# Alternating transposes and v2 products on TensorE in a fused graph attention layer, with VectorE's work in another order

## Chip, cores and metric

The kernel runs on one core of a Trainium2 chip. The metric is device time in microseconds (us) of one execution; lower is better.

## What is computed

The reference is a graph attention layer over 384 nodes with 1024 features and 16 heads of 64, with a residual:

```python
h = relu(layernorm(x))
q = h @ wq.T + bq;  k = h @ wk.T + bk;  v = h @ wv.T + bv
q2 = heads(q @ wiq.T + biq); k2 = heads(k @ wik.T + bik); v2 = heads(v @ wiv.T + biv)
scores = q2 @ k2.T / 8 + mask          # mask: from the edge list, -inf where there is no edge
out = softmax(scores) @ v2
return x + out @ wo.T + bo
```

`mask[src, dst]` is a softplus weight chosen by the edge's type.

## The kernel before

Matrices are held as a high and a low half (fp32r, or fp16 in the attention part), so that one product of the reference is three on TensorE (`mm3`: high x high, high x low, low x high). Weights arrive in 56 chunks of 512 KB: `load` issues a chunk's transfer on the queue of SyncE (SP), `split_hi` rounds it on ScalarE, `split_lo` subtracts on VectorE or GpSimd. The first 32 chunks (v, q, v2, k) are done in a stage of their own, up to about 160 us. What follows is the stage that the change touches.

It is a loop of steps `i`, in an order written out by hand; each engine does its own instructions in the order in which the code issues them. There are 48 score tiles, three (128 rows each) for each of 16 heads; tile `i` is tile `t = i % 3` of head `h = i // 3`. On its way a tile passes through these functions, each some steps behind the one before:

- `do_S`: two score products into a PSUM bank `s` (two such banks).
- `do_ttr` (VectorE): adds the mask, takes the row minimum of the negative, writes tile `e` (six buffers).
- `do_exp` (ScalarE), `do_norm` (reciprocal on VectorE; the scaling on GpSimd for `t` = 1, 2).
- Tiles with `t` = 0: `do_high` (ScalarE) and `do_low` (VectorE) write two fp16 planes and `do_turn` transposes them by a DMA on SP's queue.
- Tiles with `t` = 1, 2: `do_T` transposes on TensorE (three transposes of 128x128, bank `t`, two banks), `do_pt` takes the result to fp16 halves (high on ScalarE, low on VectorE).
- `do_A`: six v2 products of a head (fp16, 384 wide) into the one bank `a`; `do_ao` (ScalarE, then VectorE) takes them out, `do_aos` (ScalarE, then GpSimd) splits a pair of heads for the output product.

Between these, `fill` puts other products on TensorE, by a credit of 7.9 (later 8) per step. First come those of `fill_qk`: 16 chunks of q2 and k2 weights, 24 products each. When a chunk begins, `qk_head` is queued as a task and run at the end of the step: it issues a load, splits the weights two chunks on, and calls `qk_done`, which takes the finished chunk before out of PSUM (`nat`: ScalarE high, VectorE low) and issues four DMAs on SP's queue. Then come the products of `fill_o`, the output matrix: six groups (a half row of a node tile each), each in two halves of k with one bank `g` per half (three banks, taken in turn; two groups of the second half use bank `s`). `ysum` adds a finished half to the residual on VectorE and so frees its bank; `flush_y` issues the sums that are due. `OREADY` is the earliest step for the products of a k. `wo_prep` splits a chunk of the output weights in the steps of `WSTEPS`.

Of the kernel before, what the change touches and what calls it, by code (L numbers as in the profile page):

```python
# [1 line left out]

# [23 lines left out]
def gnn_kernel(ctx: ExitStack, tc: tile.TileContext, x, edges, erows, etw, wq, wk, wv, wiq, wik, wiv, wo,  # L26
# [20 lines left out]
    def bank(tag):  # L47
        return psum.tile([128, 512], F32, tag=tag, name=tag, bufs={"g": 3, "a": 1}.get(tag, 2))
# [14 lines left out]
    def load(w):  # L63
        if w >= NCH:
            return
        n, m = chunks[w]
        raw[w] = wpool.tile([128, D], F32, tag="raw", name="raw", bufs=4)
        nc.sync.dma_start(raw[w], W[n][m])

    def split_hi(w, dst=None, dve=False):  # L70
        if w >= NCH:
            return
        if dst is None:
            t = wpool.tile([128, 2, D], F32R, tag="whl", name="whl", bufs=4)
            dst = (t[:, 0, :], t[:, 1, :])
        whl[w] = dst
        if dve:
            nc.vector.tensor_copy(dst[0], raw[w])
        else:
            nc.scalar.activation(dst[0], raw[w], AF.Copy)  # L80

    def split_lo(w, eng=None):
        if w < NCH:
            hi, lo = whl[w]
            (eng or nc.vector).tensor_tensor(lo, raw[w], hi.bitcast(F32), OP.subtract)  # L85
# [155 lines left out]
    def mask_select(g):  # L241

        nc.vector.copy_predicated(ma, mbt[g].bitcast(I32), mbt[g])
# [148 lines left out]
    w = 0  # L392
# [203 lines left out]
            tasks.pop(0)()  # L596

    def qk_head(w):
        first = w - W0 < 3
        if not first:  # L600
            load(w + 5)
            split_hi(w + 2)
        if pendq:
            pendq.pop(0)()
        if 0 < w - W0 < NTAB:
            mask_select(w - W0)
        if first:
            split_hi(w + 2)
        split_lo(w + 2, nc.gpsimd if (w + 2) % 2 == PAR else None)
        if first:  # L610
            load(w + 5)
        if w == W0:
            mask_select(0)

# [17 lines left out]
    W0 = 32  # L632
    WO = NCH - 8

    LT, LA = 5, 7
    DT = (0,)
    PRE, RATE, RATE_O, RATE_E = 84, 7.9, 8, 8
    WSTEPS = (37, 40, 42, 44, 47, 51)
# [17 lines left out]
    def omm(t, h, k, c=(0, 512)):  # L656
        hi, lo = (a[:, h * 512 + c[0]:h * 512 + c[1]] for a in whl[WO + k])
        mm3(oacc[t, h][:, c[0]:c[1]], ao[:, 0, k, t * 128:(t + 1) * 128], ao[:, 1, k, t * 128:(t + 1) * 128],
            hi, lo, k in (0, KH), k in (KH - 1, KT - 1))

    OT = [(0, 0), (0, 1), (1, 0), (1, 1), (2, 0), (2, 1)]
    OREADY = 17
    now = [-1]
    wready = [0, 0] + [99] * 6

    def ysum(a, c=(0, 512)):
        t, h = OT[a]
        y = xb[t][:, h * 512 + c[0]:h * 512 + c[1]]
        nc.vector.tensor_tensor(y, oacc[t, h][:, c[0]:c[1]], y, OP.add)
        return y  # L670

    ysums = []

    def flush_y():
        while ysums:
            ysum(ysums.pop(0))

    def fill_o():


        first = [(0, 0), (0, 1), (1, 0), (1, 1), (2, 0), (2, 1)]
        first += [(a, k) for k in (2, 3) for a in range(3)] + [(a, k) for a in range(3, 6) for k in range(KH)]
        for a, k in first:
            while now[0] < wready[k] or now[0] < 6 * k + OREADY:
                yield 0
            if k == 0:
                flush_y()
                oacc[OT[a]] = bank("g")
            omm(*OT[a], k)
            if k == KH - 1:  # L690
                ysums.append(a)
            yield 4
        bank_step = (0, 0, 0, 49, 50)
        todo = [(a, k) for k in range(KH, 7) for a in range(5)]
        while todo:
            ready = [q for q in todo if now[0] >= max(6 * q[1] + OREADY, wready[q[1]], bank_step[q[0]])]
            if not ready:
                yield 0
                continue
            a, k = ready[0]  # L700
            todo.remove(ready[0])
            if k == KH:
                flush_y()
                oacc[OT[a]] = bank("gggss"[a])
            omm(*OT[a], k)
            yield 4

    st_ps, es, sts, tps, avs, aof = {}, {}, {}, {}, {}, {}
    S = 48

    def do_S(i):
        h, t = divmod(i, 3)
        p, o = divmod(h, 2)
        qs, ks = stacks["q", p], stacks["k", p]
        ps = st_ps[i] = bank("s")
        for s in range(2):
            nc.tensor.matmul(ps[:, :N], qs[:, o, t * 128:(t + 1) * 128], ks[:, o, s, :], start=(s == 0), stop=(s == 1))  # L717
# [7 lines left out]
    def do_exp(i):  # L725
        s = sts[i]
        nc.scalar.activation(es[i], es[i], AF.Exp, bias=s[:, 0:1], scale=-1.0, accum_out=s[:, 1:2])  # L727
# [20 lines left out]
    def do_high(i):  # L748
        planes[i] = plv[i // 3 % 3]
        nc.scalar.activation(planes[i][:, 0, :], es[i], AF.Copy, scale=sts[i][:, 2:3])  # L750

    def do_low(i):
        pl = planes[i]
        nc.vector.scalar_tensor_tensor(pl[:, 1, :], es.pop(i), sts[i][:, 2:3], pl[:, 0, :], op0=OP.mult, op1=OP.subtract)  # L754
# [3 lines left out]
        nc.sync.dma_start_transpose(ptv[h % 3][:, :, t * 128:(t + 1) * 128],  # L758
                                    planes.pop(i).rearrange("p a n -> p (a n)"))

    def do_T(i):
        ps = tps[i] = bank("t")
        for k in range(3):
            nc.tensor.transpose(ps[:, k * 128:(k + 1) * 128], es[i][:, k * 128:(k + 1) * 128], ident)  # L764

    def do_pt(i):
        h, t = divmod(i, 3)
        pt = ptv[h % 3]
        hi, lo = (pt[:, s * 3:s * 3 + 3, t * 128:(t + 1) * 128] for s in range(2))
        pv = tps.pop(i)[:, :N].rearrange("p (k n) -> p k n", k=3)  # L770
        nc.scalar.activation(hi, pv, AF.Copy, scale=PSC)  # L771
        nc.vector.scalar_tensor_tensor(lo, pv, PSC, hi, op0=OP.mult, op1=OP.subtract)  # L772

    def do_A(h):
        p, o = divmod(h, 2)
        ps = avs[h] = bank("a")
        for k in range(3):
            for s in range(2):
                nc.tensor.matmul(ps[:, :N], vhl[:, k, h, :, :], ptv[h % 3][:, 3 * s + k, :],  # L779
                                 start=(k == 0 and s == 0), stop=(k == 2 and s == 1))  # L780

    def do_ao(h):
        p, o = divmod(h, 2)
        if o == 0:
            aof[p] = work.tile([128, N], F32, tag="aof", name="aof")
        tmp = work.tile([128, N], F32, tag="aot", name="aot", bufs=1)
        ps = avs.pop(h)
        m, l = slice(o * 64, o * 64 + 64), slice(64 - o * 64, 128 - o * 64)
        nc.scalar.activation(tmp[m, :], ps[l, :N], AF.Identity, scale=down[l], bias=bc[m, 40 + p:41 + p])
        nc.vector.scalar_tensor_tensor(aof[p][m, :], ps[m, :N], down[m], tmp[m, :], op0=OP.mult, op1=OP.add)  # L790

    def do_aos(h):
        p = h // 2
        nc.scalar.activation(ao[:, 0, p, :], aof[p], AF.Copy)
        nc.gpsimd.tensor_tensor(ao[:, 1, p, :], aof[p], ao[:, 0, p, :].bitcast(F32), OP.subtract)
# [4 lines left out]
    def fill(n):  # L800
        credit[0] += n
        while credit[0] > 0 and gens:
            try:
                c = next(gens[0])
            except StopIteration:
                gens.pop(0)
                continue
            if c == 0:
                credit[0] = 0.0
                return  # L810
            credit[0] -= c
# [1 line left out]
    fill(PRE)  # L813
    pt_setup()
    wp = 2
    for i in range(S + LA + 4):
        now[0] = i
        r = RATE if len(gens) == 2 else RATE_O if i < S else RATE_E
        fill(r / 2)
        if i < S:  # L820
            do_S(i)
        fill(r / 2)
        if 0 <= i - 1 < S:
            do_ttr(i - 1)
        flush_y()
        if 0 <= i - 2 < S:
            do_exp(i - 2)
        if 0 <= i - 3 < S:
            do_norm(i - 3)
            if (i - 3) % 3 in DT:  # L830
                do_high(i - 3)
        if 0 <= i - LT < S and (i - LT) % 3 not in DT:
            do_T(i - LT)
        j = i - LA
        if j >= 2 and (j - 2) % 3 == 0 and (j - 2) // 3 < 16:
            do_A((j - 2) // 3)
        if 0 <= i - 4 < S and (i - 4) % 3 in DT:
            do_low(i - 4)
        if 0 <= i - LT - 1 < S and (i - LT - 1) % 3 not in DT:
            do_pt(i - LT - 1)  # L840
        if j >= 3 and (j - 3) % 3 == 0 and (j - 3) // 3 < 16:
            do_ao((j - 3) // 3)
        if j >= 4 and (j - 4) % 6 == 3:
            do_aos((j - 4) // 3)
        run_tasks()
        if 0 <= i - 4 < S and (i - 4) % 3 in DT:
            do_turn(i - 4)
        if i in WSTEPS:
            wo_prep(wp)
            wready[wp] = i + 2  # L850
            wp += 1
    while gens:
        now[0] = 999
        fill(999)


    def finish(a, c=(0, 512)):
# [51 lines left out]
```

## Time and profile before

| | |
|---|---|
| median of 3 runs | 297.39 us (297.25 to 299.25) |
| profiled execution | 297.12 us |
| its span, first to last instruction | 295.4 us |
| TensorE matmul, weight load | 287.1, 264.6 us busy |
| VectorE | 214.9 us busy |
| ScalarE | 160.4 us busy |
| GpSimd | 155.6 us busy |
| granted TensorE clock | 1.000 |

In the profile PE is TensorE's matmul, PEld its weight load, DVE VectorE, ACT ScalarE, POOL GpSimd, SP SyncE. A row of a timeline gives the start in us from the beginning of the span, the time taken, engine, source line, operation, what is written and read, shapes and count; in brackets stands the engine's idle time before it and what ended it. Rows of a source line or tile give the shortest, median and longest duration in ns. Matmuls are pipelined: one starts before the one ahead of it has ended, so their spacing is read from the starts.

### The profile page before, as it was taken

How to read it: one execution, taken by the hardware profiler on the slowest of the kernel's cores; microseconds unless marked ns; L12 is line 12 of the kernel's file. 1: busy time of each engine (PE TensorE's matmuls, PEld its weight loads, DVE VectorE, ACT ScalarE, POOL GpSimd, SP SyncE). 2: the span in 40 equal slices, each digit the busy share in tenths (PEclk: the TensorE clock that was granted, in tenths of full speed). 3: DMA queues.
4: the chain of work that ended last, by engine and by line, in shares of the span. 5: the costliest groups of instructions: out<-in, count | busy, mean ns of one | idle time of the engine just before them, and what ended most of it. 6: DMA issues, size and time to landing. Idle time of an engine off the chain costs nothing.

```text
span 295.4 us, 4837 instructions
## 1 busy us (share of the span) xinstructions
PE 287.1 (97%) x1610; PEld 264.6 (90%) x1610; DVE 214.9 (73%) x509; ACT 160.4 (54%) x291; POOL 155.6 (53%) x153
## 2 busy tenths in 40 slices
PE   6999999999999999999999999999999999989995
PEld 5999999999988889999999999898999998758774
DVE  4958986667754453999875778888888878598723
ACT  3884644234422124335635668787878777459510
POOL 4766666445766888990023445362635357475310
PEclk9999999999999999999999999999999999999999
DMA  7799867982464331386449999777788867811105
GB/s 270 252 327 411 288 192 266 288 279 74 145 214 141 107 118 65 89 275 233 142 126 236 255 249 202 189 175 194 181 201 179 200 159 162 213 29 27 27 2 213
DMA packets 33305, 54.60 MB, mean 185 GB/s; under 512 B 17408, under 2 KB 20992, under 8 KB 33280
## 3 DMA queue, kind: packets, MB, share of 16 engines
q1 hardware_dynamic: 30896, 51.90, 60.8%
q0 software_dynamic: 2064, 1.80, 2.1%
q10 hardware_dynamic: 320, 0.59, 0.8%
q8 instruction: 13, 0.21, 0.3%
q14 instruction: 12, 0.10, 0.1%
HBM read 38.30 MB, written 3.39 MB: 141 GB/s over the span
## 4 chain that ended last, share of the span: by engine, by line
PE 88%; ACT 5%; issue 3%; DVE 2%; DMA 1%; POOL 0%; ACTq 0%
PE g L375 20%; PE g L373 20%; PE g L374 20%; PE s L717 5%; PE a L779 5%; PE t L764 3%; PE s L375 2%; PE s L373 2%; PE s L374 2%; PE g L422 2%; PE t L375 2%; PE t L373 2%; PE t L374 2%; DMA g<-in_x_dram 1%; ACT whl L80 1%
## 5 line engine op out<-in xcount | busy, mean ns | idle before, releaser
L373 PE MATMUL g<-g,whl 128*128 128x384 f32 x312 | 106.8, 342 | 0.0
L375 PE MATMUL g<-g,whl 128*128 128x384 f32 x312 | 104.5, 335 | 0.0
L374 PE MATMUL g<-g,whl 128*128 128x384 f32 x312 | 104.3, 334 | 0.0
L230 POOL DMA_INDIRECT tab<-val,idx x51 | 58.0, 1138 | 33.4 <-issue 11.5
L80 ACT ACTIVATE whl<-raw 128x1024 fp32r<-128x1024 f32 x51 | 53.6, 1053 | 30.0 <-PE g L375 21.1
L85 DVE TENSOR_TENSOR whl<-raw,whl 128x1024 fp32r<-128x1024 f32 x41 | 54.2, 1321 | 17.4 <-ACT whl L80 15.1
L373 PEld LDWEIGHTS g<-g,whl 128*128 128x128 f32 x312 | 58.6, 188 | 0.7
L375 PEld LDWEIGHTS g<-g,whl 128*128 128x128 f32 x312 | 58.6, 188 | 0.3 <-POOL whl L85 0.3
L374 PEld LDWEIGHTS g<-g,whl 128*128 128x128 f32 x312 | 58.6, 188 | 0.0
L744 POOL TENSOR_TENSOR e<-e,s 128x384 f32<-128x384 f32 x32 | 27.6, 864 | 39.0 <-DVE s L740 37.5
L85 POOL TENSOR_TENSOR whl<-raw,whl 128x1024 fp32r<-128x1024 f32 x11 | 26.5, 2411 | 36.8 <-ACT whl L80 33.3
L389 ACT ACTIVATE g<-f,bc 128x384 fp32r<-128x384 f32 x24 | 14.8, 618 | 53.5 <-DVE f L388 39.6
L727 ACT ACTIVATE e<-e,s 128x384 f32<-128x384 f32 x48 | 29.2, 607 | 8.7 <-DVE s L723 7.6
L723 DVE CUSTOM_DVE_ANT_0 e<-s,ma 128x384 f32<-128x384 f32 x48 | 26.4, 551 | 3.0 <-PE s L717 3.0
L717 PE MATMUL s<-ks,qs 128*128 128x384 f32 x96 | 25.1, 342 | 2.3 <-DVE s L723 2.3
L388 DVE TENSOR_TENSOR f<-g,rrow 128x384 f32<-128x384 f32 x24 | 13.3, 553 | 18.0 <-PE g L375 12.0
L717 PEld LDWEIGHTS s<-ks,qs 128*128 128x128 f32 x96 | 17.0, 188 | 5.0 <-DVE s L723 4.2
L384 DVE SCALAR_TENSOR_TENSOR nat<-g,bc,nat 128x384 fp32r<-128x384 f32 x16 | 9.9, 617 | 14.7 <-ACT nat L383 13.6
L754 DVE SCALAR_TENSOR_TENSOR pt<-e,s,pt 128x384 f16<-128x384 f32 x16 | 19.0, 1187 | 1.4 <-ACT pt L750 0.2
L772 DVE SCALAR_TENSOR_TENSOR pt<-t,pt 128x384 f16<-128x384 f32 x32 | 17.4, 544 | 1.9 <-ACT pt L771 1.9
L779 PE MATMUL a<-pt,vhl 128*128 128x384 f16 x96 | 18.2, 326 | 0.0
L390 DVE SCALAR_TENSOR_TENSOR g<-f,bc,g 128x384 fp32r<-128x384 f32 x24 | 16.7, 700 | 0.7 <-ACT g L389 0.7
(166 smaller groups left out, 446.3 us busy)
## 6 DMA issues: line engine op xcount, KB each, us to landing
ks<-nat SPq DMA_DIRECT2D x30, 192.0 KB
raw<-in_wv_dram SPq DMA_DIRECT2D x8, 512.0 KB
raw<-in_wq_dram SPq DMA_DIRECT2D x8, 512.0 KB
raw<-in_wiv_dram SPq DMA_DIRECT2D x8, 512.0 KB
raw<-in_wk_dram SPq DMA_DIRECT2D x8, 512.0 KB
raw<-in_wiq_dram SPq DMA_DIRECT2D x8, 512.0 KB
raw<-in_wik_dram SPq DMA_DIRECT2D x8, 512.0 KB
raw<-in_wo_dram SPq DMA_DIRECT2D x8, 512.0 KB
```

The costliest lines, as they stand in the source:

```text
L80: nc.scalar.activation(dst[0], raw[w], AF.Copy)
L85: (eng or nc.vector).tensor_tensor(lo, raw[w], hi.bitcast(F32), OP.subtract)
L230: nc.gpsimd.indirect_dma_start(out=tabs[c // RNG], out_offset=bass.IndirectOffsetOnAxis(ap=idx[:, c:c + 1], axis=0), in_=val[:, c:c + 1], ...
L373: nc.tensor.matmul(ps, lhi, rhi, start=first, stop=False)
L374: nc.tensor.matmul(ps, lhi, rlo, start=False, stop=False)
L375: nc.tensor.matmul(ps, llo, rhi, start=False, stop=last)
L717: nc.tensor.matmul(ps[:, :N], qs[:, o, t * 128:(t + 1) * 128], ks[:, o, s, :], start=(s == 0), stop=(s == 1))
L723: nc.vector.tensor_tensor_reduce(e, st_ps.pop(i)[:, :N], ma[:, t, :], -0.125, 3.0e38, OP.add, OP.min, s[:, 0:1])
L727: nc.scalar.activation(es[i], es[i], AF.Exp, bias=s[:, 0:1], scale=-1.0, accum_out=s[:, 1:2])
L744: nc.gpsimd.tensor_tensor(es[i], es[i], s[:, 2:3].to_broadcast([128, N]), OP.mult)
L754: nc.vector.scalar_tensor_tensor(pl[:, 1, :], es.pop(i), sts[i][:, 2:3], pl[:, 0, :], op0=OP.mult, op1=OP.subtract)
L779: nc.tensor.matmul(ps[:, :N], vhl[:, k, h, :, :], ptv[h % 3][:, 3 * s + k, :], start=(k == 0 and s == 0), stop=(k == 2 and s == 1))
```

## The change

Tiles 3h+1 and 3h+2 are both transposed in step 3h+7 (before: 3h+6 and 3h+7), and the v2 products of the head before, which move from step 3h+6 to 3h+7 of this count, are issued in turn with them: transpose, product, transpose, product, six of each. The last head keeps the steps it had. `do_pt` for both tiles and `do_ao` follow in the step after. `do_low` moves ahead of `do_exp` and `do_norm`. The sums of output groups are issued one at a time, just before the bank that they free is taken again, rather than all in the step in which they are due. In `qk_head`, `qk_done` comes first, then the split, and the load last, for every chunk (before: for the first three alone). `OREADY` rises by one.

```diff
     def qk_head(w):
-        first = w - W0 < 3
-        if not first:
-            load(w + 5)
-            split_hi(w + 2)
         if pendq:
             pendq.pop(0)()
         if 0 < w - W0 < NTAB:
             mask_select(w - W0)
-        if first:
-            split_hi(w + 2)
+        split_hi(w + 2)
         split_lo(w + 2, nc.gpsimd if (w + 2) % 2 == PAR else None)
-        if first:
-            load(w + 5)
+        load(w + 5)
...
-    LT, LA = 5, 7
...
-    OREADY = 17
+    OREADY = 18
...
-    def flush_y():
-        while ysums:
+    def flush_y(n=6):
+        for _ in range(min(n, len(ysums))):
             ysum(ysums.pop(0))
...
             if k == 0:
-                flush_y()
+                flush_y(1)
                 oacc[OT[a]] = bank("g")
...
             if k == KH:
-                flush_y()
+                flush_y(1)
                 oacc[OT[a]] = bank("gggss"[a])
...
-    def do_T(i):
+    def turn_mm(i):
         ps = tps[i] = bank("t")
         for k in range(3):
             nc.tensor.transpose(ps[:, k * 128:(k + 1) * 128], es[i][:, k * 128:(k + 1) * 128], ident)
+            yield
...
-    def do_A(h):
-        p, o = divmod(h, 2)
+    def av_mm(h):
         ps = avs[h] = bank("a")
         for k in range(3):
             for s in range(2):
                 nc.tensor.matmul(ps[:, :N], vhl[:, k, h, :, :], ptv[h % 3][:, 3 * s + k, :],
                                  start=(k == 0 and s == 0), stop=(k == 2 and s == 1))
+                yield
+
+    def turns_and_av(tiles, heads):
+        a, b = ([g(x) for x in xs] for g, xs in ((turn_mm, tiles), (av_mm, heads)))
+        a, b = (itertools.chain(*x) for x in (a, b))
+        end = object()
+        while True:
+            x, y = next(a, end), next(b, end)
+            if x is end and y is end:
+                return
...
+    t_at, a_at = {}, {}
+    for h in range(16):
+        for t in (1, 2):
+            t_at.setdefault(3 * h + 7 if h < 15 else 3 * h + 5 + t, []).append(3 * h + t)
+        a_at[3 * h + 10 if h < 15 else 3 * h + 9] = h
-    for i in range(S + LA + 4):
+    for i in range(S + 11):
...
             do_ttr(i - 1)
-        flush_y()
+        if 0 <= i - 4 < S and (i - 4) % 3 in DT:
+            do_low(i - 4)
         if 0 <= i - 2 < S:
             do_exp(i - 2)
         if 0 <= i - 3 < S:
             do_norm(i - 3)
             if (i - 3) % 3 in DT:
                 do_high(i - 3)
-        if 0 <= i - LT < S and (i - LT) % 3 not in DT:
-            do_T(i - LT)
-        j = i - LA
-        if j >= 2 and (j - 2) % 3 == 0 and (j - 2) // 3 < 16:
-            do_A((j - 2) // 3)
-        if 0 <= i - 4 < S and (i - 4) % 3 in DT:
-            do_low(i - 4)
-        if 0 <= i - LT - 1 < S and (i - LT - 1) % 3 not in DT:
-            do_pt(i - LT - 1)
-        if j >= 3 and (j - 3) % 3 == 0 and (j - 3) // 3 < 16:
-            do_ao((j - 3) // 3)
-        if j >= 4 and (j - 4) % 6 == 3:
-            do_aos((j - 4) // 3)
+        turns_and_av(t_at.get(i, []), [a_at[i]] if i in a_at else [])
+        for x in t_at.get(i - 1, []):
+            do_pt(x)
+        if i - 1 in a_at:
+            do_ao(a_at[i - 1])
+        if a_at.get(i - 2, 0) % 2:
+            do_aos(a_at[i - 2])
         run_tasks()
...
     while gens:
         now[0] = 999
         fill(999)
+    flush_y()
```

More of the change, by code (lines that the diff above doesn't have):

```diff
@@ L1 @@
+import itertools
 from contextlib import ExitStack
```

## Prediction

> **What bounds the kernel now.** I read the page's engine shares and the chain first, then the timeline of TensorE around every place where two starts are too far apart, then VectorE and ScalarE at those places.
>
> ```profile
> span 295.4 us, 4837 instructions
> PE 287.1 (97%) x1610; PEld 264.6 (90%) x1610; DVE 214.9 (73%) x509; ACT 160.4 (54%) x291; POOL 155.6 (53%) x153
> PE 88%; ACT 5%; issue 3%; DVE 2%; DMA 1%; POOL 0%; ACTq 0%
> ```
>
> TensorE sets the end. A change can win only by giving it less work or by taking out its gaps. The profiled execution took 297.12 us, 1.7 around its span of 295.4; the median of the runs is 297.39. My sum is made against 297.12. A measurement of this kernel tells about 1% (3.0 us) from no change.
>
> The gaps, on TensorE in order of time:
>
> ```profile
> 185.86 0.33 PE L375 MATMUL g<-g,whl 128*128 128x384 f32 x1
> 186.03 0.51 PE L717 MATMUL s<-ks,qs 128*128 128x384 f32 x2
> ...
> 189.49 0.34 PE L375 MATMUL g<-g,whl 128*128 128x384 f32 x1
> 190.24 0.61 PE L717 MATMUL s<-ks,qs 128*128 128x384 f32 x2 [0.42 <-DVE s L723]
> ...
> 203.89 0.34 PE L375 MATMUL g<-g,whl 128*128 128x384 f32 x1
> 204.65 0.61 PE L717 MATMUL s<-ks,qs 128*128 128x384 f32 x2 [0.42 <-DVE s L723]
> ...
> 218.29 0.34 PE L375 MATMUL g<-g,whl 128*128 128x384 f32 x1
> 218.53 0.62 PE L717 MATMUL s<-ks,qs 128*128 128x384 f32 x2
> ...
> 232.17 0.34 PE L375 MATMUL g<-g,whl 128*128 128x384 f32 x1
> 232.42 0.62 PE L717 MATMUL s<-ks,qs 128*128 128x384 f32 x2
> ...
> 252.63 0.40 PE L373 MATMUL g<-whl,g 128*128 128x512 f32 x1
> 253.29 0.50 PE L374 MATMUL g<-whl,g 128*128 128x512 f32 x1 [0.26 <-POOL whl L85]
> ...
> 259.00 0.51 PE L717 MATMUL s<-ks,qs 128*128 128x384 f32 x2
> 259.34 0.40 PE L373 MATMUL g<-whl,g 128*128 128x512 f32 x1
> ...
> 260.27 0.39 PE L374 MATMUL g<-whl,g 128*128 128x512 f32 x1
> 260.50 0.40 PE L375 MATMUL g<-whl,g 128*128 128x512 f32 x1
> 262.37 0.61 PE L717 MATMUL s<-ks,qs 128*128 128x384 f32 x2 [1.47 <-DVE s L723]
> ```
>
> The first column is the start. Undisturbed, what follows a 384-wide product starts 0.17 behind it (185.86 to 186.03), what follows a 512-wide one 0.23 (260.27 to 260.50), and a score pair lasts 0.51. So S was late by 190.24 - 189.49 - 0.17 = 0.58, and its pair, 0.61 long, loses 0.10 more: 0.68. Likewise 0.69, 0.18 and 0.19 at 204, 218 and 232: 1.74 together, once in six steps. At 252.6 an output product waits for a weight half from GpSimd: 0.43 + 0.10 = 0.53. At 260.5 the loss is 1.64 + 0.10 = 1.74. These are the 4.0 us that a better order could find.
>
> **Term 1, the alternation itself.** The same 96 transposes and 96 v2 products run; only their order changes. What they take now:
>
> ```profile
> 191.76 0.49 PE L764 MATMUL t<-ident,e 128*128 128x128 f32 x3
> 192.09 1.14 PE L779 MATMUL a<-pt,vhl 128*128 128x384 f16 x6
> 192.93 0.48 PE L373 MATMUL g<-g,whl 128*128 128x384 f32 x1
> 193.25 0.33 PE L374 MATMUL g<-g,whl 128*128 128x384 f32 x1
> ...
> L764 PE MATMUL t<-ident,e x96: 270/272/273, 171.5 to 278.9; 128*128 128x128 f32 x96
> ...
> L779 PE MATMUL a<-pt,vhl x96: 326/326/337, 177.7 to 282.6; 128*128 128x384 f16 x96
> ...
> L422 PE MATMUL g<-g,whl x3: 222/282/283, 11.6 to 11.8; 128*128 128x256 f32 x2, 128*128 128x128 f32 x1
> ```
>
> Three transposes take 0.33, 0.11 each, and the last of them is followed by a v2 product at the same 0.11. Six v2 products are spaced (1.14 - 0.326) / 5 = 0.163; with the product behind them, whose start is shown early and which then holds 0.32 instead of 0.17, they cost 0.84 + 0.15 = 0.99, 0.01 above 6 x 0.163. Alternating would pay if a transpose's 0.11 were a weight load that a wide product could cover. But the step from transpose to v2 product is 0.11 already, and that step stays in the new order. And a 128-column product whose load was hidden behind 256-wide ones lasts 222 ns, while even the shortest of 96 transposes, a third of which follow a wide product, lasts 270: 50 ns more than a covered load explains. So the transpose streams for 0.11, and I take 6 x 0.11 + 6 x 0.163, as before. What the rows don't show is the step from a v2 product to a transpose. Nearest is the one from v2 product to weight product, 0.01 over; from below 0. There are 14 x 5 + 2 = 72 such steps: 0 to 0.72, I take the middle, 0.36. Against that, 14 separate blocks of transposes vanish, 0.01 of edge each: -0.14. Term 1: **+0.2** (-0.14 to +0.6).
>
> The Trainium skill, "TensorE: Matmul & The Clock Gate", section "LDWEIGHTS (loading the stationary operand)", has a weight load at columns / 1.2 GHz, an estimate of 107 ns for 128 columns. By that rule 0.11 would be the load, and alternating would cover it. The same page, section "Part 4: PE-mode transpose", has transposes not raising the clock; 128 columns at half clock are an estimate of 107 ns too, and nothing would be saved. The rows above side with the second.
>
> **Term 2, the query/key stage (steps 0 to 37).** Why S waits at 189.5: VectorE, then ScalarE.
>
> ```profile
> 184.61 1.26 DVE L754 SCALAR_TENSOR_TENSOR pt<-e,s,pt 128x384 f16<-128x384 f32 x1
> 185.79 0.55 DVE L772 SCALAR_TENSOR_TENSOR pt<-t,pt 128x384 f16<-128x384 f32 x1
> 186.41 0.62 DVE L790 SCALAR_TENSOR_TENSOR aof<-a,vsc,aot 64x384 f32<-64x384 f32 x1
> 187.96 0.62 DVE L384 SCALAR_TENSOR_TENSOR nat<-g,bc,nat 128x384 fp32r<-128x384 f32 x1 [0.93 <-ACT nat L383]
> 188.49 1.22 DVE L85 TENSOR_TENSOR whl<-raw,whl 128x1024 fp32r<-128x1024 f32 x1
> 189.63 0.55 DVE L723 CUSTOM_DVE_ANT_0 e<-s,ma 128x384 f32<-128x384 f32 x1
> ...
> 185.09 0.47 ACT L771 ACTIVATE pt<-t 128x384 f16<-128x384 f32 x1
> 185.71 0.67 ACT L789 ACTIVATE aot<-a,bc,vsc 64x384 f32<-64x384 f32 x1 [0.16 <-PE a L779]
> 186.40 1.06 ACT L80 ACTIVATE whl<-raw 128x1024 fp32r<-128x1024 f32 x1
> 187.36 0.56 ACT L383 ACTIVATE nat<-g,bc 128x384 fp32r<-128x384 f32 x1
> ```
>
> One step holds low, pt, ao, nat and, for every second chunk, a split, and the score evacuation (L723) queues behind all of it. A chunk is 24 products of 7.9 per step, 3.04 steps, so its head always meets steps 1 mod 3, the step of low, pt and ao. In the new order pt and ao lie in the step behind, and nat stands ahead of the split on ScalarE. ScalarE then does nat at about 185.2 and the split from 185.7 to 186.7; VectorE ends low at 185.9, nat at 186.4, the split at 187.9, and the evacuation starts 1.7 earlier than at 189.63, against a lateness of 0.68. The chunk's last product, for which nat waits, ends at 185.86 + 0.33 now, and 1.3 earlier when the transposes and products (0.33 + 0.99, term 1) that stood ahead of it move behind this step's S; S itself is wanted when it is now, since the same block lies ahead of it. All four gaps go: **-1.74** (0 if ScalarE has to stand still for that last product ahead of nat, since the split then comes as late as now). The step behind gets pt, pt, ao: 0.55 + 0.55 + 0.62 with the evacuation's 0.55, 2.3 in a step of 1.7 (7.9 products of 0.17 and a score pair); the light step after it takes up the rest.
>
> The load moves behind four DMA issues of q and k on SP's queue and ahead of the DMA transpose as before. It is needed three chunks, over 20 us, later, so nothing waits. The v2 products come a step later, so the DMA transpose and the pt halves have more room, and the output products' gate moves by the same step (17 to 18), which bites nowhere: counted through, every output product lands in the step in which it does now. A head's second score tile is turned a step later, in the first 0.65 of the block; VectorE asks for its buffer, one of six, in the step behind that, and were it late, the evacuation would stand for the rest of a 1.65 block at most.
>
> **Term 3, the weight half at 252.6.** It is split in a step in which pt and ao now are gone from ScalarE ahead of it: at least 0.47 earlier there, about 0.4 on GpSimd, whose queue holds a scaling in between. **-0.45** (0 to -0.53).
>
> **Term 4, the output sums.** Why S waits at 260.5:
>
> ```profile
> 257.10 0.69 DVE L669 TENSOR_TENSOR res<-g,res 128x512 f32<-128x512 f32 x1 [1.05 <-PE g L375]
> ...
> 258.26 2.34 DVE L754 SCALAR_TENSOR_TENSOR pt<-e,s,pt 128x384 f16<-128x384 f32 x1
> ...
> 261.75 0.56 DVE L723 CUSTOM_DVE_ANT_0 e<-s,ma 128x384 f32<-128x384 f32 x1
> ```
>
> The third of three sums stood 1.05 at the head of VectorE's queue for its product, then came a slow low, pt and ao, and only then the evacuation. New: one sum, of a product long done; pt and ao behind the evacuation. It comes over 2 us earlier: **-1.74**.
>
> What is late next: the sum of group 1 now is queued only in step 45, just ahead of the product that wants its bank, behind a weight split of step 44. Let X be the time at which TensorE ends the block of step 43. The last v2 result is there at X + 0.16; ScalarE does pt (0.50), ao (0.69) and the split (0.97, starts 186.40 to 187.36) from X + 0.03, ending near X + 2.3; VectorE's split takes 1.15, the sum 0.69: X + 4.15. TensorE wants the bank after three output products (three times 0.23 each) and two score pairs (0.34 each): X + 2.75. **+1.4** (0.7 to 1.6; 0 is a rival). For the sums in steps 47, 49 and 50 the same walk leaves 1.5, 0.4 and 0.5 of room; a low as slow as the 2.34 above would cost up to 0.65 at the last: 0.
>
> Sum: 297.12 + 0.2 - 1.74 - 0.45 - 1.74 + 1.4 = 294.79, so **294.8 us**, 0.9% under the median shown; its own range, by the bounds of terms 1, 3 and 4, is 293.7 (-0.34, -0.08, -0.7) to 296.5 (+0.4, +0.45, +0.2, +0.65).
>
> **Rivals.**
> - The load is hidden after all: 87 alternated transposes save 50 ns each (272 less 222), 4.35, so 290.4. For it: spacing 0.11; against: the 270 minimum.
> - No wait for the bank: ScalarE runs ahead, and the 1.4 falls away: 293.4. For it: ScalarE is 54% busy; against: its pt and ao hang on TensorE.
> - The gaps only move: nat waits on ScalarE, the split stays late, and terms 2 and 3 give nothing: 294.8 + 2.2 = 297.0. For it: VectorE's work is the same, 1.05 of waiting shows that queues block; against: the 1.7 worked out.
> - Slower: the bank waits. Each of the five sums queued just ahead of its user costs 1.4 and not one only, since VectorE lags by a step: 294.8 + 4 x 1.4 = 300.4. It decides once VectorE is over 1 us later than my walk in steps 47 to 50; two such extra waits undo the gain. For it: VectorE must now be level with TensorE at five places where before it had a step of grace; against: rooms of 0.4 to 1.5.
>
> **Chances.** Forecast 0.52, load hidden 0.06, no bank wait 0.16, gaps move 0.15, bank waits 0.11. Faster by over 1% (below 294.4): 0.18 of the forecast, 0.06 and 0.16: 0.40. Slower by over 1% (above 300.4): half of the bank waits and some of what no case names: 0.09. Within: 0.51. The range leaves out the hidden load and most of the bank waits: 292.8 to 298.8.
>
> **What would show it.** Right: no gap before S between 185 and 235; transposes and v2 products at 0.11 and 0.163 to 0.17 in turn, 1.65 a block; VectorE no longer waiting in L669 before step 50; one gap of 1 to 1.5 us before the first product of group 4, released by L669. Wrong: v2 products 0.06 behind transposes; gaps before several groups' first products; ScalarE idle ahead of L383.

## The result, and the profile after

The changed kernel takes 294.5 us (median of 4 runs, 294.35 to 294.8) against 297.54 before (4 runs, 297.25 to 299.25): a ratio of 0.989, interval 0.986 to 0.992. The forecast was 294.8. The profiled executions take 294.56 and 297.12.

In some executions the work ahead of the change's loop ends about 1.6 us later (e1's profile below has its first score product at 161.9, the changed kernel's at 160.3), so kernels are compared below from their first score product to the end of the span, too. That is read from two lines of each: the span, and the score products with their first start. Before, then after:

```profile
core 0 of [0], span 295.4 us
L717 PE MATMUL s<-ks,qs x96: 331/334/445, 160.2 to 268.0; 128*128 128x384 f32 x96
```

```profile
core 0 of [0], span 292.8 us
L711 PE MATMUL s<-ks,qs x96: 333/334/346, 160.3 to 265.3; 128*128 128x384 f32 x96
```

135.2 us became 132.5, 2.7 less. The second line tells more: the three durations are shortest, median and longest in ns, and a score product that comes late is shown 0.10 longer. Before, the longest is 445; after, 346: none of the 96 score products (S) comes late any more. The page after:

```profile
PE 284.7 (97%) x1610; PEld 267.4 (91%) x1610; DVE 208.2 (71%) x509; ACT 159.7 (55%) x291; POOL 154.8 (53%) x153
```

TensorE has the same 1610 matmuls and is still 97% busy. One block of the new order, on TensorE's timeline:

```profile
185.63 0.27 PE L758 MATMUL t<-ident,e 128*128 128x128 f32 x1
185.74 0.32 PE L773 MATMUL a<-pt,vhl 128*128 128x384 f16 x1
185.90 0.27 PE L758 MATMUL t<-ident,e 128*128 128x128 f32 x1
186.01 0.33 PE L773 MATMUL a<-pt,vhl 128*128 128x384 f16 x1
...
187.10 0.33 PE L773 MATMUL a<-pt,vhl 128*128 128x384 f16 x1
187.13 0.47 PE L374 MATMUL g<-g,whl 128*128 128x384 f32 x1
187.44 0.33 PE L375 MATMUL g<-g,whl 128*128 128x384 f32 x1
```

The first two weight loads behind the start of that block:

```profile
185.64 0.10 PEld L773 LDWEIGHTS <-vhl 128*128 128x128 f16 x1
185.74 0.14 PEld L758 LDWEIGHTS t<-ident,e 128*128 128x128 f32 x1
```

From transpose to v2 product it is 0.11, from v2 product to transpose 0.16. Each load starts with the instruction ahead of its own, so a transpose's load now lies beside a wide product, and the transpose (duration 0.27, as before) still takes 0.11. That doesn't show that a transpose streams for 0.11 itself, as the prediction has it: the load of the v2 product behind it, shown at 0.10, fills the same time. No run separates the two. Either way a load stands behind each transpose in both orders, and there is nothing for the alternation to save.

The VectorE and ScalarE rows of the same step, which answer to those at 184.61 to 189.63 before:

```profile
184.43 0.62 DVE L748 SCALAR_TENSOR_TENSOR pt<-e,s,pt 128x384 f16<-128x384 f32 x1 [0.35 <-ACT pt L744]
184.97 0.16 DVE L734 RECIPROCAL s<-s 128x1 f32<-128x1 f32 x1
185.64 0.62 DVE L385 SCALAR_TENSOR_TENSOR nat<-g,bc,nat 128x384 fp32r<-128x384 f32 x1 [0.51 <-ACT nat L384]
186.58 1.23 DVE L86 TENSOR_TENSOR whl<-raw,whl 128x1024 fp32r<-128x1024 f32 x1 [0.33 <-ACT whl L81]
187.73 0.55 DVE L717 CUSTOM_DVE_ANT_0 e<-s,ma 128x384 f32<-128x384 f32 x1
...
185.02 0.58 ACT L384 ACTIVATE nat<-g,bc 128x384 fp32r<-128x384 f32 x1
185.50 1.05 ACT L81 ACTIVATE whl<-raw 128x1024 fp32r<-128x1024 f32 x1
```

The evacuation starts at 187.73 (before: 189.63; forecast: 187.9), and in these rows VectorE waits 0.35 + 0.51 + 0.33 = 1.19, where it waited 0.93 before. The new wait, on TensorE, and what VectorE and ScalarE did ahead of it:

```profile
258.37 0.51 PE L711 MATMUL s<-ks,qs 128*128 128x384 f32 x2
260.25 0.50 PE L374 MATMUL g<-whl,g 128*128 128x512 f32 x1 [1.37 <-DVE res L663]
...
257.18 0.62 DVE L794 SCALAR_TENSOR_TENSOR aof<-a,vsc,aot 64x384 f32<-64x384 f32 x1
258.27 1.23 DVE L86 TENSOR_TENSOR g<-raw,g 128x1024 fp32r<-128x1024 f32 x1 [0.46 <-ACT g L81]
259.51 0.69 DVE L663 TENSOR_TENSOR res<-g,res 128x512 f32<-128x512 f32 x1
...
255.97 0.49 ACT L766 ACTIVATE pt<-t 128x384 f16<-128x384 f32 x1 [0.32 <-PE t L758]
256.48 0.67 ACT L793 ACTIVATE aot<-a,bc,vsc 64x384 f32<-64x384 f32 x1
257.17 1.06 ACT L81 ACTIVATE g<-raw 128x1024 fp32r<-128x1024 f32 x1
```

The first product of group 4 was due 0.35 behind 258.37 and starts at 260.25: 1.53, and with the 0.11 by which it lasts longer 1.64. The row names the sum; in front of the sum stands the weight split of step 44, which waits for its high half on ScalarE.

### The profile page after: what moved, and what is told of

Read it like the earlier page. It is cut to its first block, busy times and chain, and to the rows that moved or that the text cites. A ratio compares the mean times of both kernels' runs of the same rounds, so it can differ in the third digit from the quotient of the medians.

```text
span 292.8 us, 4859 instructions
## 1 busy us (share of the span) xinstructions
PE 284.7 (97%) x1610; PEld 267.4 (91%) x1610; DVE 208.2 (71%) x509; ACT 159.7 (55%) x291; POOL 154.8 (53%) x153
## 5 line engine op out<-in xcount | busy, mean ns | idle before, releaser
L231 POOL DMA_INDIRECT tab<-val,idx x51 | 59.7, 1171 | 32.0 <-issue 11.8
L738 POOL TENSOR_TENSOR e<-e,s 128x384 f32<-128x384 f32 x32 | 26.4, 829 | 31.2 <-DVE s L734 23.0
L773 PE MATMUL a<-pt,vhl 128*128 128x384 f16 x96 | 26.1, 326 | 0.0
L758 PE MATMUL t<-ident,e 128*128 128x128 f32 x96 | 24.9, 272 | 0.0
L711 PE MATMUL s<-ks,qs 128*128 128x384 f32 x96 | 24.5, 335 | 0.0
L767 DVE SCALAR_TENSOR_TENSOR pt<-t,pt 128x384 f16<-128x384 f32 x32 | 16.6, 549 | 8.2 <-ACT pt L766 8.2
L799 POOL TENSOR_TENSOR g<-aof,g 128x384 fp32r<-128x384 f32 x8 | 8.3, 1041 | 25.5 <-ACT g L798 25.5
L744 ACT ACTIVATE pt<-e,s 128x384 f16<-128x384 f32 x16 | 9.9, 616 | 15.4 <-issue 9.4
```

Of the source, the lines that this page charges most:

```text
L231: nc.gpsimd.indirect_dma_start(out=tabs[c // RNG], out_offset=bass.IndirectOffsetOnAxis(ap=idx[:, c:c + 1], axis=0), in_=val[:, c:c + 1], ...
L738: nc.gpsimd.tensor_tensor(es[i], es[i], s[:, 2:3].to_broadcast([128, N]), OP.mult)
```

## Experiments

"Stage" is from the first score product to the end. The last column is the time that TensorE loses at stalls over 0.05 us from the first score product to step 50, added up from starts as in the prediction. Each ratio is to runs of the kernel before that were taken together with that kernel; their medians lie between 297.25 and 297.32, and at 297.54 for the changed kernel.

| kernel | us, median | ratio to before, interval | stage us | stalls us |
|---|---|---|---|---|
| before | 297.3 | | 135.2 | 4.2 |
| changed | 294.5 | 0.989 (0.986 to 0.992) | 132.5 | 1.6 |
| e1 in sequence | 295.08 | 0.989 (0.985 to 0.994) | 132.1 | 1.3 |
| e2 old head | 295.7 | 0.995 (0.993 to 0.998) | 133.6 | 2.8 |
| e3 old places | 296.2 | 0.996 (0.993 to 0.998) | 134.3 | 3.2 |
| e4 old low | 294.49 | 0.991 (0.988 to 0.994) | 132.5 | 1.6 |
| e5 sum ahead | 293.52 | 0.986 (0.982 to 0.989) | 131.5 | 0.7 |
| e6 old sums | 294.85 | 0.991 (0.988 to 0.994) | 132.6 | 1.7 |
| e7 sum ahead, in sequence | 293.37 | 0.987 (0.983 to 0.992) | 131.2 | 0.4 |
| e8 places alone | 295.98 | 0.994 (0.992 to 0.997) | 134.0 | 3.1 |
| e9 split on GpSimd | 292.98 | 0.986 (0.983 to 0.989) | 130.9 | 0 |
| e10 the same, in sequence | 292.96 | 0.985 (0.983 to 0.988) | 130.8 | 0 |
| e11 split and sum | 292.84 | 0.985 (0.982 to 0.988) | 130.8 | 0 |
| e12 low alone | 297.53 | 1.001 (0.999 to 1.003) | 135.3 | 4.3 |

**Is the alternation worth anything? (e1, e7, e10)** The edit, on the changed kernel in e1, on top of e5 in e7 and of e9 in e10 (with `and`, a v2 product is issued only once the transposes are used up):

```diff
-            x, y = next(a, end), next(b, end)
-            if x is end and y is end:
+            if next(a, end) is end and next(b, end) is end:
                 return
```

> The changed kernel, but in the common step all six transposes come first and then the six v2 products; everything else stays. Theory (order on TensorE is worth nothing, a transpose streams for 0.108 us itself): 294.4 to 294.8 us, transposes spaced 0.108, v2 products 0.163. Rival (the alternation hides the transposes' weight loads and carries part of the gain): 1 us or more slower than the changed kernel, 295.5 or above.

> The sum of step 44 ahead, and transposes and v2 products in sequence in place of alternating. Theory: as with the sum ahead alone, 292.6 to 293.0 us, 130.6 to 130.9 us from the first score product to the end. Rival (alternation is worth something once the wait behind it is gone): 0.5 us or more slower than with the sum ahead alone.

> The split of step 44 on GpSimd, and transposes and v2 products in sequence in place of alternating. Theory (the alternation is worth nothing, since a transpose streams for 0.108 us itself): within 0.3 us of the alternating one, 130.6 to 131.0 us from the first score product to the end. Rival (alternating pays once nothing else waits): 131.3 us or more.

The block in e10, on TensorE's timeline:

```profile
192.68 0.82 PE L758 MATMUL t<-ident,e 128*128 128x128 f32 x6
193.33 1.14 PE L773 MATMUL a<-pt,vhl 128*128 128x384 f16 x6
194.17 0.47 PE L374 MATMUL g<-g,whl 128*128 128x384 f32 x1
```

Start to next product 1.49 in sequence; alternating, 185.63 to 187.13, 1.50. With no stall left in either, the stages are 130.8 and 130.9. The alternation is worth nothing. While a wait is left, it even costs 0.3: the wait for the bank is 1.35 in e1 against 1.64, the late S 0.43 in e7 against 0.73 in e5. In sequence ScalarE has the transposes of both tiles sooner, and its split of step 44 begins 2.6 behind the start of the block in e1 (255.90 to 258.48), 2.9 in the changed kernel (254.30 to 257.17). The rival asked for 1 us more than the changed kernel; e1's median of 295.08 shows half of that, but its stage, 132.1, is no longer than the changed kernel's 132.5. e7's 293.37 and its stage of 131.2 lie above the range given, which took the late S of e5 to be gone.

**What freed S in the query/key stage? (e2, e3, e4, e12)** e2 puts the head back:

```diff
+        first = w - W0 < 3
+        if not first:
+            load(w + 5)
+            split_hi(w + 2)
         if pendq:
...
-        split_hi(w + 2)
+        if first:
+            split_hi(w + 2)
...
-        load(w + 5)
+        if first:
+            load(w + 5)
```

> The changed kernel with the chunk head in its old order (load, high split, then the evacuation nat). Theory (term 2: pt and ao out of the step of low free 1.17 us of VectorE there, more than the 0.68 by which S was late, so the head's order alone isn't needed): 294.4 to 295.0 us, no gap before S between 185 and 235 us. Rival (nat ahead of the split is what lets S go): the gaps of 1.74 us come back, 296.2.

My theory fell here: S is late again at 218, 225 and 232, 1.1 us together, two thirds of the rival's 1.74. VectorE and TensorE at the largest:

```profile
228.49 0.62 DVE L385 SCALAR_TENSOR_TENSOR nat<-g,bc,nat 128x384 fp32r<-128x384 f32 x1 [1.46 <-ACT nat L384]
229.02 1.22 DVE L86 TENSOR_TENSOR whl<-raw,whl 128x1024 fp32r<-128x1024 f32 x1
230.16 0.55 DVE L723 CUSTOM_DVE_ANT_0 e<-s,ma 128x384 f32<-128x384 f32 x1
...
231.74 0.62 DVE L800 SCALAR_TENSOR_TENSOR aof<-a,vsc,aot 64x384 f32<-64x384 f32 x1
232.40 0.56 DVE L723 CUSTOM_DVE_ANT_0 e<-s,ma 128x384 f32<-128x384 f32 x1
```

```profile
232.21 0.34 PE L376 MATMUL g<-g,whl 128*128 128x384 f32 x1
233.01 0.61 PE L717 MATMUL s<-ks,qs 128*128 128x384 f32 x2 [0.47 <-DVE s L723]
```

VectorE stands 1.46 for nat on ScalarE, and what comes late is not the next evacuation but the one after it, behind pt and ao, which the change put there. With the places changed, the step behind has no slack for a late split, so here nat must come first.

e3 puts the places back, without the alternation and with the gate at 17, and keeps head, low and sums:

```diff
-    OREADY = 18
+    OREADY = 17
...
-            x, y = next(a, end), next(b, end)
-            if x is end and y is end:
+            if next(a, end) is end and next(b, end) is end:
...
-            t_at.setdefault(3 * h + 7 if h < 15 else 3 * h + 5 + t, []).append(3 * h + t)
-        a_at[3 * h + 10 if h < 15 else 3 * h + 9] = h
+            t_at.setdefault(3 * h + 5 + t, []).append(3 * h + t)
+        a_at[3 * h + 9] = h
```

> The changed kernel with transposes, v2 products, pt and ao in the steps that they had before, unalternated, and the output gate at 17; head, low and sums stay as changed. If the places carry term 2: gaps before S of 0.5 to 0.7 us at every second chunk come back, and the time is 295.5 to 296.3. If head order (0.5 us earlier) and the shorter low (0.5 us) are enough alone: no gaps, 293.8 to 294.8 us, since the wait for the bank shrinks to about 0.7 us with ao already done a step earlier.

Of the 1.8 us that the stage loses against the changed kernel, S has 0.6 (0.16, 0.11 and 0.34 at 190, 204 and 231), the weight half at 252 its 0.53 again, and two banks 2.0 where the changed kernel lost 1.6 at one; the wait did not shrink to 0.7. That sums to 1.5; 14 more separate blocks at 0.01 would add 0.1, and the rest stays open. So the first answer, that the places carry it, is right in sum, but S alone got only a third.

e4 issues low where it was.

> The changed kernel with low issued where it was, behind the reciprocal and the block of transposes and products. If low's 0.69 us in place of 1.19 comes from GpSimd's scaling no longer running beside it (the reciprocal that releases the scaling stands behind low now): low is back at 1.1 to 1.2 us, and the time is 294.4 to 295.2. If the shorter low has another cause: it stays near 0.7 us, time 294.4 to 294.8.

e12 is the kernel before with low alone moved.

> The kernel before, with low alone moved ahead of the reciprocal. Theory (GpSimd's scaling, released by that reciprocal, runs beside low and doubles its time; each of the four gaps before S between 185 and 235 us hangs on VectorE's queue behind low): low at 0.62 us in place of 1.25 up to the last heads, the gaps of 0.68 and 0.69 fall to 0.2 or less, 133.5 to 134.2 us from the first score product to the end in place of 135.2, and 296.0 to 296.5 us. Rival (the gaps hang on ScalarE's order, not on low): gaps and time stay, 297.0 to 297.5 us, even if low is shorter.

Groups of low by count, total us and mean ns: before, changed, e4, e12.

```profile
L754 DVE SCALAR_TENSOR_TENSOR pt<-e,s,pt 128x384 f16<-128x384 f32 x16 | 19.0, 1187 | 1.4 <-ACT pt L750 0.2
```

```profile
L748 DVE SCALAR_TENSOR_TENSOR pt<-e,s,pt 128x384 f16<-128x384 f32 x16 | 11.0, 689 | 2.6 <-ACT pt L744 2.6
```

```profile
L748 DVE SCALAR_TENSOR_TENSOR pt<-e,s,pt 128x384 f16<-128x384 f32 x16 | 14.3, 892 | 1.7 <-ACT pt L744 0.5
```

```profile
L754 DVE SCALAR_TENSOR_TENSOR pt<-e,s,pt 128x384 f16<-128x384 f32 x16 | 12.3, 771 | 2.3 <-ACT pt L750 2.3
```

Low is shorter by 0.5 where it stands ahead of the reciprocal, as expected, and e4 brings back only part of it: neither of the two answers given for e4, because low is long in some heads and short in others (last section). e4's stage is 132.5 like the changed kernel's, and no S is late in it, so low's new place isn't needed for the gain. In e12 it buys nothing by itself: the four gaps are there at full size, and VectorE shows why.

```profile
186.37 0.62 DVE L754 SCALAR_TENSOR_TENSOR pt<-e,s,pt 128x384 f16<-128x384 f32 x1 [0.20 <-ACT pt L750]
...
189.71 0.62 DVE L384 SCALAR_TENSOR_TENSOR nat<-g,bc,nat 128x384 fp32r<-128x384 f32 x1 [0.93 <-ACT nat L383]
190.25 1.22 DVE L85 TENSOR_TENSOR whl<-raw,whl 128x1024 fp32r<-128x1024 f32 x1
191.38 0.55 DVE L723 CUSTOM_DVE_ANT_0 e<-s,ma 128x384 f32<-128x384 f32 x1
```

Low ends earlier, and nat waits for ScalarE, which still does pt, ao and the split first. Before the change the gaps hung on ScalarE's order. The rival was right; e3, where nat goes first but pt and ao stay, has 0.6 of the 1.74 left.

**What is behind the wait for the bank? (e5, e6, e8, e9, e11)** e5 adds, behind `do_ttr`:

```diff
+        if i == 44:
+            flush_y(1)
```

> The changed kernel with one more sum issued in step 44, behind the score evacuation and ahead of the weight split, so that the bank of group 4 is free when TensorE comes to it. Theory (the 1.64 us at 258.6 is the sum queued behind pt, ao and the split): the gap goes, 1.5 to 1.7 us less than the changed kernel, 292.8 to 293.0 us, and from the first score product to the end 130.8 us in place of 132.5. Rival (the stop only moves to the score evacuation or to the next bank): 294 us or more.

Half of each: 293.52 lies between the two answers. The wait for the bank is gone, and S in the same step is late by 0.73 instead, behind the same split and the next sum. e6 issues all sums when due, e8 is the kernel before with the new places, the alternation and the gate at 18 alone.

> The changed kernel with the sums all issued behind the score evacuation of the step in which they fall due, as before. Theory (with pt and ao moved and low short, VectorE can afford to wait for the products there): no bank wait and no late S, 292.8 to 293.5 us. Rival (sums one at a time are what freed S at 260.5): S is late by 0.5 us or more around step 45, 293.5 to 295 us.

> The kernel before with only the places changed: both transposes and the v2 products alternating in one step, pt and ao in the step behind, the output gate at 18; head, low and sums in their old order. From the runs so far: the gaps that the old head left (1.1 us) stay, the weight half at 252 is in time, and what S loses around step 45 decides: 133.7 us from the first score product to the end less the 1.6 of the bank wait, 132.1 us, 294.1 us in all, if the old sums cost nothing here; 295 us or more if they make S late.

In e6 the rival was right, in e8 the second answer, and in the same way: S is late by 1.73. In e8 no weight half is late, and S loses 1.3 more at 221, 227 and 235, where the head is in its old order. VectorE and TensorE in e6:

```profile
260.92 1.23 DVE L86 TENSOR_TENSOR g<-raw,g 128x1024 fp32r<-128x1024 f32 x1 [0.46 <-ACT g L81]
262.18 0.69 DVE L663 TENSOR_TENSOR res<-g,res 128x512 f32<-128x512 f32 x1
262.78 0.55 DVE L717 CUSTOM_DVE_ANT_0 e<-s,ma 128x384 f32<-128x384 f32 x1
```

```profile
261.54 0.40 PE L376 MATMUL g<-whl,g 128*128 128x512 f32 x1
263.39 0.61 PE L711 MATMUL s<-ks,qs 128*128 128x384 f32 x2 [1.46 <-DVE s L717]
```

Wherever these runs put the sums, the split of step 44 is ahead of what TensorE needs next. e9 takes only it away from VectorE:

```diff
-    PAR, OPOOL, ODVE = 1, (2, 3, 4, 6), (2,)
+    PAR, OPOOL, ODVE = 1, (2, 3, 4, 5, 6), (2,)
```

> The changed kernel, with the low half of the weight split of step 44 on GpSimd in place of VectorE (GpSimd stands idle from 257.4 to 262.1 us there). Theory (that split, 1.23 us on VectorE behind its high half on ScalarE, holds up both the sum that frees group 4's bank and the next score evacuation): no gap at group 4 and none before the score products behind it, 1.6 us less than the changed kernel, 130.8 to 130.9 us from the first score product to the end, 292.8 to 293.0 us. Rival (the sums' late issue holds TensorE by itself): 0.5 us or more of the gap stays.

> The split of step 44 on GpSimd and the sum of step 44 ahead as well. Theory: with the split gone from VectorE the sum's place no longer matters, same as with the split alone, 130.8 to 130.9 us from the first score product to the end. Rival (both are needed): 0.5 us or more below the split alone.

TensorE in e9, where the wait was, and what VectorE did:

```profile
258.43 0.51 PE L711 MATMUL s<-ks,qs 128*128 128x384 f32 x2
258.77 0.39 PE L374 MATMUL g<-whl,g 128*128 128x512 f32 x1
...
257.24 0.62 DVE L794 SCALAR_TENSOR_TENSOR aof<-a,vsc,aot 64x384 f32<-64x384 f32 x1
257.89 0.69 DVE L663 TENSOR_TENSOR res<-g,res 128x512 f32<-128x512 f32 x1
```

The product comes 0.34 behind S: no wait. The stage falls by 1.6, all of it, and e11 is no faster. e9 is the version to keep: one number in a list, 1.4% under the kernel before and 1.5 us under the changed one.

## Why the prediction was right, by its steps

- Term 1, the alternation, +0.2: measured 0. The step from transpose to v2 product stayed 0.11, which the prediction read from three transposes with a product behind them. The 0.005 taken for each change back was too much: 0.16 is the plain v2 spacing. That a transpose streams for 0.11 is not shown: the durations that the prediction compares (270 against 222 ns) speak for it, but the 222 is a product's. No run shows a half clock (the mean granted clock is 1.000 before and after). The term needs neither: if the 0.11 were a load, alternating would still have saved nothing, since the v2 product behind each transpose has a load of its own.
- Term 2, the four gaps, -1.74: all gone. The walk put the evacuation at 187.9, it came at 187.73. e2 and e3 each lose part of it, so the prediction was right to take both edits together; that the head's order wouldn't be needed was my later error. What the walk didn't know is that low would be 0.5 shorter; e12 shows that this alone moves nothing, and e4 that the gain doesn't need it.
- Term 3, the weight half, -0.45: -0.53, none of that wait is left; e3 has it again with pt and ao back, and e8 is without it with only the places changed.
- Term 4, the late S at 260.5, -1.74: gone. The prediction put it to the sums and to a slow low of 2.34; no run takes away one of them alone (in e12 low stays at 2.43 there, in e6 the split of step 44 is in the way instead). The wait for group 4's bank, +1.4: 1.64, just over the bound of 1.6, at the place and behind the instructions that were named. ScalarE's split began at 257.17, and the sum ended near 260.2.
- Not in the sum: the small late S at 265, 0.20, is gone too. -1.74 - 0.53 - 1.74 - 0.20 + 1.64 = -2.57 of the 2.7 by which the stage fell; fewer separate blocks, 0.14 by the prediction's own rate, are nearest to the rest, which was not tested by itself. That the forecast came within 0.3 is in part luck: the 0.24 that the bank's wait cost beyond the sum offsets part of what terms 1 and 3 and the S at 265 gave beyond it.
- Of the rivals, a saving by hidden weight loads is excluded by e10, the missing bank wait by the row at 260.25, and that the gaps only move by the four that are gone. Gaps before several groups did not come: one bank of five waited.

## What to carry to other kernels

When an engine is full and the profile shows it waiting, follow the queue of the engine that it waits for back to the instruction that itself waits: here it was ScalarE's order in the query/key stage before, and one weight split after. A shorter instruction in front of such a wait (e12) or another place for the last link (e5, e6) only moves the stop; taking the long instruction out of the queue (e9) ends it. Read the spacing of mixed instruction kinds from the starts before building an alternation for it.

## What the runs showed of the hardware

VectorE's low took 0.62 us alone and up to 1.27 beside GpSimd's scaling of 0.83, as at 184.61 before (1.26), where GpSimd had:

```profile
184.63 0.83 POOL L744 TENSOR_TENSOR e<-e,s 128x384 f32<-128x384 f32 x1 [0.49 <-DVE s L740]
```

In the prediction I took 1.26 for the instruction's own time. The slow low of 2.34 at 258.26 before stands beside a weight split of 2.39 on GpSimd that began at 257.79. Scaling and split read SBUF, and low reads two operands there, the tile and the high plane. The Trainium skill, "SBUF — State Buffer", section "Who interferes with whom", says that a VectorE instruction with two SBUF inputs contends with a GpSimd instruction that reads SBUF, through a shared read port, and one blocks the other. The runs agree: in e4 low takes these two forms in neighbouring heads, with and without a scaling beside it.

```profile
191.36 0.62 DVE L748 SCALAR_TENSOR_TENSOR pt<-e,s,pt 128x384 f16<-128x384 f32 x1
...
197.91 1.19 DVE L748 SCALAR_TENSOR_TENSOR pt<-e,s,pt 128x384 f16<-128x384 f32 x1
...
197.86 0.83 POOL L738 TENSOR_TENSOR e<-e,s 128x384 f32<-128x384 f32 x1 [0.85 <-DVE s L734]
```

Where low was already running, it was GpSimd that took longer: before, low at 166.48 took 0.60, and the scaling that began at 166.65 took 1.12.
